# A decoder's last step: routed rows added by index DMAs into the residual, in place of VectorE adds

## The chip, the core and the metric

The kernel runs on one core of a Trainium2 chip. The core has TensorE (PE, matrix multiply), VectorE (DVE, elementwise), ScalarE (ACT, activation functions), GpSimd (POOL, which here makes the index DMAs), and SyncE (SP, which issues plain DMAs). Sixteen DMA engines move data between the chip's main memory and the on-chip memory, whatever queue a transfer was issued on. The metric is the device time of one execution in microseconds (us), as the median of several runs.

## The reference

The program is a two-layer decoder over x of shape (8, 256, 256) in float32: self-attention, cross-attention and a feed-forward part, twice, each added to the residual x. Only the very last part is touched, the second layer's feed-forward part, a mixture of eight experts of which each token uses one, beside a shared expert that all tokens use:

```python
def _L1_ffn_ref(x_bsD, router_DE, w1_eDF, w3_eDF, w2_eFD, ws1_DF, ws3_DF, ws2_FD):
    x_aD = x_bsD.reshape(a, d)
    scores_aE = x_aD @ router_DE
    vals_aK, idx_aK = jax.lax.top_k(scores_aE, K)          # K = 1
    masked_aE = jnp.full_like(scores_aE, -jnp.inf).at[jnp.arange(a)[:, None], idx_aK].set(vals_aK)
    gates_Ea = jax.nn.sigmoid(masked_aE).T
    routed_in_EaD = gates_Ea[:, :, None] * x_aD[None, :, :]
    mid_EaF = silu(einsum('ead,edf->eaf', routed_in_EaD, w1_eDF)) * einsum('ead,edf->eaf', routed_in_EaD, w3_eDF)
    routed_out_EaD = jnp.einsum('eaf,efd->ead', mid_EaF, w2_eFD)
    shared_aD = (silu(x_aD @ ws1_DF) * (x_aD @ ws3_DF)) @ ws2_FD
    return (shared_aD + routed_out_EaD.sum(axis=0)).reshape(b, s, d)

x = x + _L1_ffn_ref(_layernorm(x, axis=-1), ...)
```

So each output row is the sum of three things: the residual row, the shared expert's row, and the row of the one expert to which the token was routed.

## The kernel before

The 2048 tokens are held as 16 tiles of 128 rows by 256 columns, all in one on-chip tile `x` of shape [128, 16, 256]; `x[:, j, :]` is tile j, 128 KB. It is the residual for the whole program. `plain` (line 158) is the program for all ordinary inputs; `token_experts` (line 1740) is its last phase and holds the change.

Routing comes first. The tokens' rows, normalized and multiplied by their gates, are written into the tile `xg` (`gated`, line 1782), and index DMAs on the POOL queue (`put_rows`, line 1842) scatter them to the buffer `xs` in main memory, sorted by expert. The integer table `pos_i` holds for every token the row in that buffer. `slots` (line 1954) then runs the experts over 17 tiles of sorted rows, and `outof` (line 1938) stores each tile's result to `ye` (called `ys` in the profile) from the ScalarE queue. The rows of `ye` are in the sorted order, so that they have to be gathered by `pos_i` to go back to their tokens.

The shared expert runs in four quarters of 512 tokens. For a quarter q, `hidden_shared` makes the hidden activations `mid` in six chunks of up to 128 features (TensorE, then a SiLU on ScalarE at line 1161, then a product on VectorE at line 1162), and `joined(q, mid, i)` (line 1768) multiplies 128 of the tokens out (TensorE, line 1759) and adds the result from the accumulators into `x[:, 4 * q + i, :]` on VectorE (line 1770). Quarters 0 to 2 are done well before; quarter 3 (tiles 12 to 15) is kept to the end, so that TensorE has work while the last expert's rows go out to `ye` and come back.

The end of the program, lines 1985 to 2011, is then this. Sixteen gathers (line 1993, index DMAs on the POOL queue) bring the routed rows of tiles 12, 13, 14, 15, 0, 1, ... 11, in this order, into `xg`, which is free again. All of them wait for the last store to `ye`. On VectorE an order written out by hand runs in four groups: four adds of `xg[:, j, :]` into `x[:, j, :]` (line 2005), then one `joined`. Group 0 adds tiles 12 to 15 and joins tile 12; groups 1, 2, 3 add tiles 0 to 3, 4 to 7, 8 to 11 and join tiles 13, 14, 15. Stores to the output go out on SP: one of four tiles, 512 KB, after the adds of groups 1 to 3 (line 2008), and one of a single tile, 128 KB, after each join (line 2010).

`tc.issue_after(last.ins)` keeps VectorE's instructions of this block behind the last product of quarter 3's hidden activations; it binds instructions on VectorE alone. `tc.manual_schedule(engines=...)` keeps the order in which the program is written on the engines named; on the others a scheduler orders the instructions.

Of the kernel before, what the change touches and what calls it, by code (L numbers as in the profile page):

```python
# [34 lines left out]
ALU = mybir.AluOpType  # L35
# [122 lines left out]
def plain(  # L158
# [4 lines left out]
    nc = tc.nc  # L163
# [6 lines left out]
    x = const.tile([P, NT, D], F32, name="x")  # L170
# [1569 lines left out]
    def token_experts(phase):  # L1740
# [15 lines left out]
        def outward(mid, w2, lo):  # L1756
            ps = mm.tile([P, 2 * D], F32, tag="mm", name="out")[:, :D]
            for i in range(NFC):
                nc.tensor.matmul(ps, mid[:, i, lo : lo + P], w2[:, i, :], start=i == 0, stop=i == NFC - 1)
            return ps  # L1760


        def quarter(q):
            for last in hidden_shared(q, pair, silu):
                pass
            return mid_s[q % 2], last

        def joined(q, mid, i):
            xt = x[:, 4 * q + i, :]
            nc.vector.tensor_tensor(xt, xt, outward(mid, ws2, i * P), ALU.add)  # L1770
# [5 lines left out]
        xg = one.tile([P, NT, D], F32, name="xg")  # L1776
# [208 lines left out]
        ov = out.rearrange("b (t p) d -> (b t) p d", p=P)  # L1985
# [3 lines left out]
        with tc.manual_schedule(engines={mybir.EngineType.PE}):  # L1989
            mid, last = quarter(3)  # L1990
        places = [*range(12, NT), *range(12)]
        for j in places:
            nc.gpsimd.indirect_dma_start(
                out=xg[:, j, :],
                out_offset=None,
                in_=ye[:, :],
                in_offset=bass.IndirectOffsetOnAxis(ap=pos_i[:, j : j + 1], axis=0),
            )

        stored = []  # L2000
        with tc.issue_after(last.ins), tc.manual_schedule(engines={mybir.EngineType.DVE}):
            for i in range(4):
                group = places[4 * i : 4 * i + 4]
                for j in group:
                    nc.vector.tensor_tensor(x[:, j, :], x[:, j, :], xg[:, j, :], ALU.add)  # L2005
                if i:
                    lo = group[0]
                    stored.append(nc.sync.dma_start(ov[lo : lo + 4].rearrange("t p d -> p t d"), x[:, lo : lo + 4, :]))
                joined(3, mid, i)
                stored.append(nc.sync.dma_start(ov[12 + i], x[:, 12 + i, :]))  # L2010
        return stored

    with ExitStack() as phase:
        stored = token_experts(phase)
# [939 lines left out]
```

## Time and profile before

| | us |
|---|---|
| median of 3 runs | 1145.45 (1143.05 to 1147.83) |
| the profiled execution, its own time | 1145.63 |
| its span, first to last instruction | 1143.9 |
| TensorE busy in the span | 1100.9 (96%) |
| VectorE busy | 575.6 (50%) |
| GpSimd busy | 419.3 (37%) |
| the end: first gather issued, after the span's start | 1108.61 |
| the end: last matmul's end | 1134.92 |
| the end: last VectorE instruction, start | 1136.19 |
| the end: last store issued | 1136.97 |

The profile is of one execution. Its times count from the span's start. An engine is busy while it executes; issuing a DMA is not counted as busy for SP and ScalarE, whose DMA issues appear as SPq and ACTq rows in the timeline with the time that the issue took. For POOL the row of an index DMA is the time in which it makes the descriptors. The transfers themselves are seen only in the share of time for which the sixteen DMA engines are busy and in the GB/s that they move. Idle time is put down to what released it.

### The profile page before, as it was taken

The numbers are of one execution on the slowest core, as the hardware profiler recorded it, in microseconds if no ns is written. First come the engines' busy times: TensorE is split into PE (matmuls) and PEld (weight loads), VectorE is DVE, ScalarE is ACT, GpSimd is POOL, SyncE is SP. The second block draws the span as 40 slices with busy tenths as digits, with TensorE's granted clock in tenths as the row PEclk, the third lists the DMA queues.
The fourth block names the chain that finished last, engine by engine and source line by source line (L and its number), as shares of the span: only waits on it lengthen the run. The fifth ranks groups of instructions, "written<-read, shape, count | busy, mean of one in ns | idle before, by whom it ended". The sixth has DMA issues, their size and how long they took to land. (4 is left out here: it accounts for less than half of the span.)

```text
span 1143.9 us, 33749 instructions
## 1 busy us (share of the span) xinstructions
PE 1100.9 (96%) x14706; PEld 702.4 (61%) x14706; DVE 575.6 (50%) x1573; ACT 447.2 (39%) x703; POOL 419.3 (37%) x480
## 2 busy tenths in 40 slices
PE   6979999999999999999999999999999999999996
PEld 3434455555555445667676667676765668888864
DVE  5557889899877446334334243433235572222213
ACT  4657676665444524232323232323233320322220
POOL 3437365546678323242323323242425132000013
PEclk9989999999999999999999999999999999999998
DMA  8082333222004200101010101010121044999924
GB/s 247 2 272 89 105 106 96 86 98 73 18 12 168 84 3 20 39 20 39 20 39 20 39 20 39 20 40 19 40 77 38 1 177 183 387 410 387 367 66 132
DMA packets 52253, 117.15 MB, mean 102 GB/s; under 512 B 8816, under 2 KB 37216, under 8 KB 47744
## 3 DMA queue, kind: packets, MB, share of 16 engines
q1 hardware_dynamic: 45920, 99.17, 25.6%
q0 software_dynamic: 3456, 12.73, 3.0%
q10 hardware_dynamic: 2720, 3.02, 0.7%
q8 instruction: 117, 1.92, 0.7%
q14 instruction: 40, 0.33, 0.1%
HBM read 104.26 MB, written 27.93 MB: 116 GB/s over the span
## 5 line engine op out<-in xcount | busy, mean ns | idle before, releaser
L341 ACT ACTIVATE pT<-st 128x1024 f32<-128x1024 f32 (+1 forms) x128 | 110.5, 915 | 73.9 <-PE st L330 70.0
L367 PE MATMUL o<-pT,padv 128*32 128x256 f32 (+1 forms) x1536 | 96.4, 367 | 7.1 <-DVE by_q L383 5.6
L272 PE MATMUL h<-xrT,w 128*64 128x128 f32 (+1 forms) x1936 | 87.2, 250 | 2.3 <-issue 2.3
L1527 POOL TENSOR_TENSOR both<-pTx 128x512 f32<-128x512 f32 x64 | 80.8, 1291 | 23.1 <-ACT pTx L1525 19.1
L272 PEld LDWEIGHTS h<-xrT,w 128*64 128x64 f32 x1936 | 84.5, 137 | 5.3 <-issue 3.1
L341 ACT ACTIVATE pT<-st,kbias 128x1024 f32<-128x1024 f32 x64 | 67.9, 1112 | 35.9 <-PE st L330 35.9
L1162 DVE TENSOR_TENSOR midr<-sl,h 128x128 f32<-128x128 f32 x102 | 29.4, 288 | 103.5 <-PE h L272 70.8
L367 PEld LDWEIGHTS o<-pT,padv 128*32 128x32 f32 x1536 | 44.6, 110 | 54.6 <-issue 19.1
L1525 ACT ACTIVATE pTx<-stx 128x1024 f32<-128x1024 f32 x64 | 62.1, 1022 | 31.9 <-PE stx L1521 31.9
L1161 ACT ACTIVATE sl<-h 128x128 f32<-128x128 f32 (+1 forms) x114 | 35.4, 310 | 96.8 <-PE h L272 57.8
L330 PE MATMUL st<-qm,kT 32*128 32x512 f32 (+1 forms) x512 | 66.7, 589 | 3.9 <-DVE seq L513 2.2
L254 POOL TENSOR_TENSOR lnrs<-lnve,mhalf 128x2 f32<-128x2 f32 x48 | 36.0, 752 | 91.8 <-DVE lnve L252 85.0
L278 PE MATMUL qk<-xnT,l_wqkv 128*32 128x256 f32 x1024 | 66.9, 383 | 0.0
L1521 PE MATMUL stx<-qTx,kTx 64*128 64x256 f32 x512 | 64.3, 391 | 2.5 <-ACT pTx L1525 2.5
L1561 PE MATMUL ox<-pTx,vx 128*32 128x256 f32 x1024 | 62.3, 380 | 0.0
L1616 POOL TENSOR_TENSOR oT<-oT,rs 128x512 f32<-128x512 f32 x30 | 37.7, 1287 | 66.6 <-DMA rs<-rd 66.6
L1521 PEld LDWEIGHTS stx<-qTx,kTx 64*128 64x128 f32 x512 | 46.1, 186 | 20.7 <-ACT pTx L1525 7.2
L272 PE MATMUL wo<-wout_x,oT 128*64 128x256 f32 x512 | 58.0, 379 | 0.0
L346 POOL TENSOR_SCALAR_AFFINE_SELECT pT<-pT 128x512 f32<-128x512 f32 x64 | 42.1, 673 | 40.6 <-ACT pT L341 40.3
L254 POOL TENSOR_TENSOR lxrs<-lxve,mhalf 128x2 f32<-128x2 f32 x8 | 5.6, 706 | 133.4 <-DVE sc L1300 103.4
L1569 DVE COPY oT<-ox 128x512 f32<-128x512 f32 x16 | 11.1, 691 | 78.9 <-PE ox L1561 78.9
L383 DVE STREAM_TRANSPOSE by_q<-o 128x512 f32<-128x512 f32 x48 | 34.0, 708 | 33.0 <-PE o L367 33.0
(365 smaller groups left out, 2179.6 us busy)
## 6 DMA issues: line engine op xcount, KB each, us to landing
w<-packs SPq DMA_DIRECT2D x22, 1408.0 KB
w<-packs SPq DMA_DIRECT2D x22, 768.0 KB
rs<-rd SPq DMA_DIRECT2D x16, 512.0 KB
packs<-L_ffn_w_eDF SPq DMA_DIRECT2D x8, 704.0 KB
packs<-L_ffn_w_eDF SPq DMA_DIRECT2D x8, 640.0 KB
packs<-L_ffn_w_eFD SPq DMA_DIRECT2D x8, 640.0 KB
wkv_x<-L_xattn_Wkv POOLq DMA_DIRECT2D x1, 4096.0 KB
ctxT<-ctx_T SPq DMA_DIRECT2D x8, 512.0 KB
```

The costliest lines, as they stand in the source:

```text
L254: nc.gpsimd.tensor_tensor(rs[:, :n], ve[:, :n], mhalf[:, :n], ALU.pow)
L272: nc.tensor.matmul(out[h], lhsT[:, h], rhs, start=start, stop=stop, skip_group_check=True)
L278: nc.tensor.matmul(out[h : h + HP], lhsT[:, h : h + HP], rhs, start=start, stop=stop, skip_group_check=True)
L330: nc.tensor.matmul(st[:, r, :, :n], self.kT[rows, c, bass.ts(kt, P)], self.qm[rows, :, c, q0:], start=True, stop=True,)
L341: nc.scalar.activation(pT[:, :, :, :n], st[:, 2 * k : 2 * k + 2, :, :n], AF.Exp, scale=self.scale, **kb)
L346: nc.gpsimd.affine_select(out=pT[:, :, :, :P], in_=pT[:, :, :, :P], compare_op=ALU.is_ge, fill=0.0, base=0, pattern=[[0, 2], [0, 2], [1, P ...
L367: nc.tensor.matmul(o[HP * j : HP * j + HP, m, q0:], self.v_pad[:, kt, 8 * c + 2 * j + m, :], pTs[j // 2][:, j % 2, m, : S - q0], start=kt ...
L1521: nc.tensor.matmul(st[:, g, kt, :], kT[rows, c, bass.ts(kt, P)], qT[rows, c, :], start=True, stop=True)
L1525: nc.scalar.activation(pT, st, AF.Exp, scale=scale)
L1527: nc.gpsimd.tensor_tensor(both, pT[:, :, 0, :], pT[:, :, 1, :], ALU.add)
L1561: nc.tensor.matmul(o[at : at + HP, i, :], v[:, kt, 2 * (c2 + i) + g, lo : lo + HP], pT[:, g, kt, :], start=kt == 0, stop=kt == 1, skip_gro ...
L1616: engines[c2 % 4 // 2].tensor_tensor(oT[:, c2 : c2 + 2, :], oT[:, c2 : c2 + 2, :], rs[:, c2 : c2 + 2, :], ALU.mult)
```

## The change

The sixteen gathers get an operation: each adds the rows that it brings to what lies in its destination, and the destination is now the residual tile `x[:, j, :]` itself, no longer `xg[:, j, :]`. The sixteen adds on VectorE are removed; VectorE's block holds only the four joins. The stores keep their sizes. Each four-tile store now depends on the four gathers of its tiles and no longer on VectorE, and the order of SP's instructions is written out: tiles 0 to 3, then 12, then 4 to 7, then 13, then 8 to 11, then 14, then 15. The order of the gathers on the POOL queue is unchanged.

```diff
         places = [*range(12, NT), *range(12)]
         for j in places:
             nc.gpsimd.indirect_dma_start(
-                out=xg[:, j, :],
+                out=x[:, j, :],
                 out_offset=None,
                 in_=ye[:, :],
                 in_offset=bass.IndirectOffsetOnAxis(ap=pos_i[:, j : j + 1], axis=0),
+                compute_op=ALU.add,
             )
 
         stored = []
-        with tc.issue_after(last.ins), tc.manual_schedule(engines={mybir.EngineType.DVE}):
-            for i in range(4):
-                group = places[4 * i : 4 * i + 4]
-                for j in group:
-                    nc.vector.tensor_tensor(x[:, j, :], x[:, j, :], xg[:, j, :], ALU.add)
-                if i:
-                    lo = group[0]
-                    stored.append(nc.sync.dma_start(ov[lo : lo + 4].rearrange("t p d -> p t d"), x[:, lo : lo + 4, :]))
-                joined(3, mid, i)
-                stored.append(nc.sync.dma_start(ov[12 + i], x[:, 12 + i, :]))
+
+        def shared_rows(i):
+            joined(3, mid, i)
+            stored.append(nc.sync.dma_start(ov[12 + i], x[:, 12 + i, :]))
+
+        def other_rows(lo):
+            stored.append(nc.sync.dma_start(ov[lo : lo + 4].rearrange("t p d -> p t d"), x[:, lo : lo + 4, :]))
+
+        with tc.issue_after(last.ins), tc.manual_schedule(engines={mybir.EngineType.DVE, mybir.EngineType.SP}):
+            other_rows(0)
+            shared_rows(0)
+            other_rows(4)
+            shared_rows(1)
+            other_rows(8)
+            shared_rows(2)
+            shared_rows(3)
         return stored
```

## The prediction

> **What bounds the kernel now.** I read the engines' busy times first, then the chain of waits, then the end of the program in the timeline and in stretches of two microseconds. Everything the change touches lies after 1108 us, so only the last 36 us of the span can move.
>
> ```profile
> span 1143.9 us, 33749 instructions
> PE 1100.9 (96%) x14706; PEld 702.4 (61%) x14706; DVE 575.6 (50%) x1573; ACT 447.2 (39%) x703; POOL 419.3 (37%) x480
> by line: DVE x L1770 0.5%; DVE x L2005 0.5%; issue 0.2%
> ```
>
> TensorE bounds the program as a whole, but the chain that ended last consists of VectorE's adds (line 2005) and joins (line 1770): behind TensorE's last matmul VectorE is late. The chain stops at VectorE's last instruction at 1136.6, though the span ends at 1143.9; the 7.3 us between hold the stores, which the timeline shows:
>
> ```profile
> 1124.40 10.52 PE L1759 MATMUL out<-ws,mid 128*128 128x256 f32 x48
> ...
> 1126.24 1.51 POOL L1993 DMA_INDIRECT xg<-ys,pos_i  x1 [0.30 <-issue]
> 1128.06 0.95 POOL L1993 DMA_INDIRECT xg<-ys,pos_i  x1 [0.31 <-issue]
> 1131.16 0.42 DVE L1770 TENSOR_TENSOR x<-x,out 128x256 f32<-128x256 f32 x1 [3.90 <-PE out L1759]
> 1131.50 1.42 DVE L2005 TENSOR_TENSOR x<-x,xg 128x256 f32<-128x256 f32 x4
> 1131.61 0.35 SPq L2010 DMA_DIRECT2D out<-x  x1
> ...
> 1136.19 0.41 DVE L1770 TENSOR_TENSOR x<-x,out 128x256 f32<-128x256 f32 x1
> 1136.30 0.58 SPq L2008 DMA_DIRECT2D out<-x  x1
> 1136.97 2.03 SPq L2010 DMA_DIRECT2D out<-x  x1
> ```
>
> To be seen here: TensorE ends at 1124.40 + 10.52 = 1134.92, the last join starts only at 1136.19, and no store leaves before 1131.61, because SP's stores stand behind VectorE. Then the stretches (columns: PE, PEld, DVE, ACT, POOL busy, granted clock, DMA share, GB/s):
>
> ```profile
> 1110.00:1120.00 10.00, 10.00 (x24) 4.38 (x24) 1.85 (x3) 1.79 (x3) 7.56 (x9) 1.00 0.36 105
> 1120.00:1130.00 10.00, 10.00 (x37) 6.84 (x36) 2.93 (x7) 1.19 (x2) 7.17 (x7) 1.00 0.35 102
> 1130.00:1132.00 2.00, 2.00 (x11) 1.75 (x10) 0.84 (x3) 0.00 (x0) 0.00 (x0) 1.00 0.08 31
> 1132.00:1134.00 2.00, 2.00 (x11) 1.77 (x10) 2.00 (x7) 0.00 (x0) 0.00 (x0) 1.00 0.27 89
> 1134.00:1136.00 2.00, 0.93 (x5) 0.47 (x3) 2.00 (x7) 0.00 (x0) 0.00 (x0) 1.00 1.02 333
> 1136.00:1138.00 2.00, 0.00 (x0) 0.00 (x0) 0.60 (x2) 0.00 (x0) 0.00 (x0) 1.00 1.04 344
> ```
>
> From 1134 on the DMA engines are full (share 1.0) at 333 to 344 GB/s, while from 1110 to 1134 they are a third busy or less. So the end is bound by 2.1 MB of stores that start late.
>
> Last, the price of a gather now (median and range of a line's instructions, in ns) and what its data costs the engines:
>
> ```profile
> L1993 POOL DMA_INDIRECT xg<-ys,pos_i x16: 946/949/1508, 1108.6 to 1128.1; - x16
> L2005 DVE TENSOR_TENSOR x<-x,xg x16: 414/416/419, 1125.8 to 1135.9; 128x256 f32<-128x256 f32 x16
> q0 software_dynamic: 768, 2.10, 34.2%
> ```
>
> POOL makes a gather in 0.95 us and starts one every 1.254 us (0.95 and the 0.30 of issue). The last line is the gathers' queue between 1110 and 1131: 34.2% of 21 us is 7.2 us of all sixteen engines, 0.45 us a gather. The last gather is issued at 1128.06 and its data is in by 1130.5, 2.45 us later.
>
> **The change part by part.** The sum is made against the profiled execution: span 1143.9, own time 1145.63, which is 0.2 above the median shown (1145.45).
>
> The adds. Sixteen of 0.42 us start 0.335 apart and leave VectorE. Four (tiles 12 to 15) lay under TensorE's matmuls and cost nothing. The other twelve lie between the joins: each group of four with its join takes 1.67 us, three groups run from 1131.50 to 1136.60. Without them the last join waits only for TensorE's 1134.92: start about 1135.03, 1.16 us earlier. The first join still waits for TensorE until 1131.16; I keep that.
>
> The stores of tiles 0 to 3. The eighth gather is issued at 1117.48 and lands near 1119.9, so SP sends 512 KB near 1120, when the DMA engines are about 65% free, and not at 1132.95. This store moves ahead of tile 12's on SP's queue; what stands behind it there (tile 12) waits for its join until 1131.6 anyway. At 338 GB/s (the mean of the two full stretches) it is 1.55 us less in the backlog.
>
> The other stores. SP is in order: tile 12 at 1131.6 (join), 4 to 7 at 1132.0, tile 13 at 1132.5, 8 to 11 at 1132.9, tile 14 at 1133.4 (an issue takes 0.35 to 0.41 where the queue isn't full), tile 15 at 1135.5. The wait that is added is tile 4's to 7's behind tile 12's join: no loss against 1134.85 before. Data follows an issue by about 0.8 us. From 1132.4 the five stores before the last, 1.44 MB, take 4.3 us, to 1136.7; the last adds 0.4: 1137.1. By itself the last one, issued at 1135.5, would need until 1137.3 (the first store before took 1.4 to 1.8). Before, by the same arithmetic, 1.97 MB in one piece from 1133.7 end at 1139.5. Gain: 2.2 to 2.4 us; what follows (receipts, SP's closing waits) is the same in both.
>
> The gathers' new price is not shown by this trace: no DMA here adds. From below it is that of a plain gather, 0.95; a gain in it would only come from the adds no longer running beside POOL (the gather at 1126.24, issued while they ran, took 1.51), at most 0.56 us on a stream that has slack. From above I take twice, with the issue gap kept: cadence 2.2, or 2.5 if the gap doubles too. What the sum makes of it: with cadence c the last gather lands at T = 1108.61 + 15c + 2.45, and behind it go the stores of 8 to 11, 14 and 15 in SP's order: 0.1 + 0.8 + 0.79 MB / 338 GB/s = 3.2 us. Now T is 1129.9, so T + 3.2 = 1133.1, under the 1137.2 of the stores. It stays hidden up to c = 1.53, takes the gain away at 1.68 and makes the kernel 0.5% slower at 2.06.
>
> Here two rules stand against the change. The nearest rows of the trace are POOL's plain loads by size:
>
> ```profile
> L1893 POOL DMA_DIRECT2D xr<-xs x17: 536/538/597, 956.7 to 1054.5; - x17
> L809 POOL DMA_DIRECT2D wout_x<-L_xattn_Wout x1: 955/955/955, 360.0 to 360.0; - x1
> ```
>
> The first moves 128 rows of 1 KB, the second 1024: 896 rows more cost 0.42 us, 0.06 per 128. By that an extra read descriptor per row is nearly free: about 1.0, c = 1.31, all hidden. The Trainium skill, "DMA: Bandwidth & Descriptors", section "SWDGE vs HWDGE vs iDMA", says that a GpSimd core computes a pair of descriptors, one read and one write, for each operation; "Collectives: The Full Stack", section "The bandwidth ceiling", says that an add in the DMA needs two source reads, so two read descriptors per chunk, and halves the rate. Three descriptors for two, if all of the 0.95 scales: 1.42, an estimate, c = 1.73, T = 1137.0, end 1140.2, 0.7 us slower than before (own time 1146.3). I take a value near the trace's rows, at or below 1.2 (c up to 1.5), because they scale so weakly; but an index gather costs 0.41 more than a plain load of the same rows, so its work per row is not free, and the rule stays in the range.
>
> For the data, halved rate makes 0.45 into 0.9 us per gather, an estimate from that page; it fits into 1.254, together with the early store (0.9 x 16 + 1.55 = 16 us of the 20 us stream). It would bound the stream beyond 2.8 times (1.254 / 0.45).
>
> Sum: 1145.63 - 2.3 = 1143.3.
>
> **The rivals.**
> A, as above: 1143.3, bound by TensorE's last matmul and the stores behind it. For it: the idle DMA engines from 1110 to 1134 and the 4 us of slack. Its own range is 1141 to 1146.
> B, POOL becomes the bound: making an adding index gather costs about double. T = 1108.61 + 33 + 2.45 = 1144.1, end 1147.3, 7.8 us after 1139.5: 1153.4; with c = 2.5, 1157.9. For it: 0.95 us for 128 rows, so POOL is already busy three quarters of this stretch and has no second engine to help; sixteen instructions multiply any surcharge. It decides from 2.06, that is 0.8 us more per gather. Against it: how little POOL's loads grow with rows.
> C, the adds are slow in the DMA engines, or each gather must wait for the one before to land (c at least 2.45): read, add and write back of 1 KB rows. From 4.6 times the data cost (2.06 / 0.45), or by the wait, 1152 to 1158 or beyond. Against: the gathers have different tiles as destinations, and now up to two are in flight with no wait beyond reuse.
> D, nothing gained: the early store and the earlier join are hidden, or the early store does not leave early because SP's first wait is satisfied late; then only the join's 1.2 us or nothing: 1144.5 to 1145.6.
>
> **How the numbers follow.** A measurement of this kernel can tell about 0.5%, 5.7 us, from no change. A's gain of 2.3 us lies within that. Chances: A 0.43, D 0.10, B 0.34, C 0.09, and 0.04 for more than 5.7 us of gain, for which the end holds no place (the whole from TensorE's last matmul to the span's end is 9 us, of which most is a join, a store's flight and the closing). So faster 0.04, within 0.53, slower 0.43. The range runs from A with 2.8 us to spare, 1140.5, to B with c = 2.5, 1158.5; below it lies 0.04, above it about 0.13.
>
> **What would show it.** Right: POOL's rows of line 1993 at most 1.2 us and started within 1.53 of each other; the first SP store near 1120; four joins and no other VectorE work after 1126, the last starting near 1135.0; the DMA share full from about 1132.5 to 1137. Wrong: rows of line 1993 above 1.7 us, or gaps between them ended by DMAs, and the store of tiles 8 to 11 issued after 1138, long after the last matmul. If the rows are short and the DMA share between 1110 and 1130 is near 1, it is C.

## The result, and the profile after

| | before | after |
|---|---|---|
| median of 12 runs each, us | 1146.89 | 1151.28 |
| ratio after / before, 95% interval | | 1.0041 (1.0028 to 1.0054) |
| profiled execution: own time / span, us | 1145.63 / 1143.9 | 1150.11 / 1148.4 |
| last matmul's end, us of the span | 1134.92 | 1135.03 |
| from there to the span's end, us | 9.0 | 13.4 |

The changed kernel is slower by 4.4 us, where 2.3 us of gain had been forecast. TensorE ends at the same place in both profiles; the whole loss lies behind it. First the page's span and busy times of the changed kernel, and its chain of waits in the window from 1130 to 1150:

```profile
span 1148.4 us, 33744 instructions
PE 1102.7 (96%) x14706; PEld 702.9 (61%) x14706; DVE 571.0 (50%) x1557; ACT 447.3 (39%) x703; POOL 427.5 (37%) x480
...
by line: POOL x L1993 35.9%; issue 8.8%; POOLq L79 0.1%
```

VectorE does 4.6 us less, POOL 8.2 more, and the chain that ended last, VectorE's adds and joins before, is now POOL's gathers alone (shares of the window). The timeline of the changed kernel's end (start, length, engine, line, operation, and in brackets the idle time before it and what ended it):

```profile
1108.71 1.66 POOL L1993 DMA_INDIRECT x<-ys,pos_i  x1 [52.73 <-DMA ys<-yr]
1110.68 1.57 POOL L1993 DMA_INDIRECT x<-ys,pos_i  x1 [0.30 <-issue]
...
1124.51 10.52 PE L1759 MATMUL out<-ws,mid 128*128 128x256 f32 x48
...
1125.70 0.41 SPq L2008 DMA_DIRECT2D out<-x  x1
1127.30 0.42 DVE L1770 TENSOR_TENSOR x<-x,out 128x256 f32<-128x256 f32 x1 [1.28 <-DMA x<-ys,pos_i]
...
1133.28 0.38 SPq L2008 DMA_DIRECT2D out<-x  x1
1133.76 0.82 SPq L2005 DMA_DIRECT2D out<-x  x1
1134.74 1.55 POOL L1993 DMA_INDIRECT x<-ys,pos_i  x1 [0.30 <-issue]
1135.07 0.42 DVE L1770 TENSOR_TENSOR x<-x,out 128x256 f32<-128x256 f32 x1 [2.17 <-PE out L1759]
1136.59 1.55 POOL L1993 DMA_INDIRECT x<-ys,pos_i  x1 [0.30 <-issue]
1141.10 0.38 SPq L2008 DMA_DIRECT2D out<-x  x1
1141.58 1.44 SPq L2005 DMA_DIRECT2D out<-x  x2
```

To be seen: VectorE is no longer late (the last join starts at 1135.07, 0.04 behind TensorE), but POOL still makes gathers when TensorE is done. The last is issued at 1136.59, 8.5 us later than before, and the store of tiles 8 to 11 can leave only at 1141.10. The stores of tiles 14 and 15, whose rows were complete by 1135.5, stand behind it on SP's queue. The first store leaves at 1125.70.

The gathers themselves: the group's row (ns, shortest/median/longest), the landing line of the view of tile x (us from issue to landing), and the gathers' DMA queue between 1100 and 1150 (packets, MB, share of all sixteen DMA engines):

```profile
L1993 POOL DMA_INDIRECT x<-ys,pos_i x16: 1537/1547/1661, 1108.7 to 1136.6; - x16
DMA to landing us min/median/max: 3.9/4.8/5.7
...
q0 software_dynamic: 2304, 2.10, 30.5%
```

A row costs 1.547 us where it cost 0.949, and with the unchanged 0.30 of issue one starts every 1.85 us. The queue now needs 2304 packets for the sixteen gathers' 2.10 MB, about 0.9 KB each, where before 768 packets carried the same bytes, 2.7 KB each. Its share, 30.5% of 50 us for sixteen gathers, is 0.95 us of all engines per gather, where it was 0.45. The landing takes longer too: the first profile of the kernel before gives no such line, but a later one of the same kernel (the third, below) has

```profile
DMA to landing us min/median/max: 2.7/2.8/4.1
```

The stretches of the changed kernel (PE, PEld, DVE, ACT, POOL busy, clock, DMA share, GB/s):

```profile
1134.00:1136.00 2.00, 1.03 (x5) 0.57 (x3) 0.42 (x1) 0.00 (x0) 1.70 (x2) 1.00 0.96 278
...
1138.00:1140.00 2.00, 0.00 (x0) 0.00 (x0) 0.00 (x0) 0.00 (x0) 0.14 (x1) 0.81 0.78 111
1140.00:1142.00 2.00, 0.00 (x0) 0.00 (x0) 0.00 (x0) 0.00 (x0) 0.00 (x0) 0.50 0.07 12
1142.00:1144.00 2.00, 0.00 (x0) 0.00 (x0) 0.00 (x0) 0.00 (x0) 0.00 (x0) 0.50 1.00 338
```

Before, the DMA engines were full with stores from 1134 to 1138 and beyond. Now they bring the last gathers until about 1140, stand almost empty until SP is released and its first data moves, and are full with the last stores only from 1142.

Behind the stores come the closing instructions of each queue. They have rows too, though the chain of waits does not show them; a DRAIN is one of them. First before, then after:

```profile
L2950 POOLq DRAIN  x3: 46/103/4402, 1132.4 to 1143.6; - x3
L2950 SPq DRAIN  x3: 7/7/13, 1143.0 to 1143.3; - x3
```

```profile
L2957 POOLq DRAIN  x3: 46/103/4402, 1142.6 to 1148.1; - x3
L2957 SPq DRAIN  x3: 7/7/13, 1147.5 to 1147.8; - x3
```

POOL's first DRAIN takes 4.40 us. It starts after POOL's last rows have landed: at 1132.4 before, so it was over by 1136.8, under the stores; at 1142.6 after, so it is over at 1147.0. SP's first DRAIN, which closes the stores, comes at 1143.0 and 1147.5. So in the changed kernel two chains end within half a microsecond of each other, one through the stores and one through POOL's own closing.

### The profile page after: what moved, and what is told of

The parts are those of the page before. It is cut to its first block, busy times and chain, and to the rows that moved or that the text cites. A ratio compares the mean times of both kernels' runs of the same rounds, so it can differ in the third digit from the quotient of the medians.

```text
span 1148.4 us, 33744 instructions
## 1 busy us (share of the span) xinstructions
PE 1102.7 (96%) x14706; PEld 702.9 (61%) x14706; DVE 571.0 (50%) x1557; ACT 447.3 (39%) x703; POOL 427.5 (37%) x480
## 4 chain that ended last, share of the span: by engine, by line
PE 84%; DVE 6%; ACT 3%; issue 2%; POOL 1%; SPq 1%; DMA 1%; POOLq 0%; ACTq 0%; DVEq 0%
PE h L272 7%; PE st L330 7%; PE k L272 6%; PE v L272 6%; PE wo L272 5%; PE o L367 5%; PE ox L1561 5%; PE stx L1521 5%; PE out L1942 4%; PE qk L278 3%; PE h L1169 3%; PE q L272 3%; PE out L1759 3%; PE ao L278 2%; ACT pT L341 2%
```

## The experiments

Every ratio below is to the kernel before, timed on the same chip in the same set of runs.

The theory after the result: the adding operation itself costs the time, by POOL's longer rows and the later landing; leaving out VectorE's adds and sending stores early costs nothing. The rivals: the new order of SP's queue is at fault; it is adding into `x`, with stores and joins beside it; or it is the stores' start alone, which another order on SP would mend.

**The change without the add.** The only edit to the changed kernel:

```diff
                 in_offset=bass.IndirectOffsetOnAxis(ap=pos_i[:, j : j + 1], axis=0),
-                compute_op=ALU.add,
```

> The changed kernel with the add taken out of the gathers: they overwrite the residual tiles, so the residual and shared sums of tiles 0 to 11 and the residual of tiles 12 to 15 are left out of the output. Everything else (VectorE's four joins, SP's written order, early stores) is as changed. Theory 1 (POOL's price for an adding gather is the whole loss): line 1993 back at 0.95 us and one every 1.25 us, the last landed near 1130.5, last store issued near 1135.5, about 2.3 us less than before: ratio 0.997 to 0.999. Theory 2 (SP's written order and the early stores lose the time): still 3 to 5 us slower than before, ratio 1.003 to 1.004.

Measured: 1143.26 us (22 runs) against 1143.27 of before, ratio 0.9993 (0.9982 to 1.0003). The rows of line 1993 are back at 0.946 us, and the end is in this profile 5.8 us behind TensorE:

```profile
1117.38 0.41 SPq L2007 DMA_DIRECT2D out<-x  x1
...
1121.49 10.52 PE L1759 MATMUL out<-ws,mid 128*128 128x256 f32 x48
```

The first store leaves at 1117.38, before the last stage, as the prediction wanted it. So the whole loss goes with the adding operation, and the order on SP's queue costs nothing. But the early stores and the missing adds do not bring 2.3 us either.

**VectorE's adds kept, gathers plain, order changed.** The edit to the kernel before: the sixteen adds stay, but those of tiles 0 to 7 stand ahead of the second join and SP's order is written out. Here `other_rows` holds the four adds of its tiles ahead of their store. The loop that is replaced and the helpers are left out of this cut:

```diff
+        with tc.issue_after(last.ins), tc.manual_schedule(engines={mybir.EngineType.DVE, mybir.EngineType.SP}):
+            add_rows(range(12, NT))
+            shared_rows(0)
+            other_rows(0)
+            other_rows(4)
+            shared_rows(1)
+            other_rows(8)
+            shared_rows(2)
+            shared_rows(3)
```

> Plain gathers into xg and VectorE's sixteen adds kept, but stores and adds reordered: adds of tiles 12 to 15, join 12, adds and stores of 0 to 7, join 13, adds and store of 8 to 11, joins 14 and 15; SP in the same order. Theory 1: POOL is back at 1.25 us a gather, the adds lie under TensorE's last matmuls, the last join starts near 1135.0 and the stores before it have drained: 2 to 3 us less than before, ratio 0.997 to 0.999. Theory 2: stores that leave earlier and in a written order cost time, so no gain or a loss, ratio 1.000 or more.

Measured: 1143.36 us, ratio 0.9996 (0.9985 to 1.0008); the end is 5.9 us behind TensorE. Getting VectorE out of the way needs no adding DMA, but there is nothing measurable to be had from it.

**Adding gathers into the separate buffer, VectorE's adds kept.** The edit to the kernel before:

```diff
                 in_offset=bass.IndirectOffsetOnAxis(ap=pos_i[:, j : j + 1], axis=0),
+                compute_op=ALU.add,
```

> The kernel before with one part of the change alone: the gathers add, but into xg (which still holds the gated rows, so the output has these in addition); VectorE's sixteen adds and the old order of stores stay. Theory 1: 1.55 us and one every 1.85 us on POOL, the last landed near 1141, VectorE's last group and the last join wait for it, the last store leaves near 1143 and the kernel is 0.5 to 2 us slower than the changed one: ratio to before 1.004 to 1.008. Theory 2 (the written order of SP and the early stores are the loss): as fast as before, 0.999 to 1.001.

Measured: 1151.50 us against 1145.75, ratio 1.0041 (1.0028 to 1.0053), the same as the change's. So with the rows added into `xg` in place of `x`, with VectorE's adds kept and with the old order of stores, the loss is the same. In the same set the changed kernel, run again,

> The changed kernel again, beside the variants. Theory 1 (POOL's descriptors for an adding gather, then the last gather's landing, the stores of tiles 8 to 11, 14 and 15, and POOL's own closing after it): the end from the last matmul's end to the span's end is again 13 to 13.5 us. If the kernel before usually has an end of 6 to 7 us, the ratio is 1.0055 to 1.0065; if it has 9 us, 1.004.

gave 1.0035 (1.0024 to 1.0047), with its end again 13.4 us behind TensorE (1137.50 to 1150.9), and the kernel before against itself,

> The kernel before, profiled a second time. In its first profile VectorE's first join of the end waited for TensorE until 1131.16, 4 us after that product's twelve matmuls were through, while in the changed kernel and in both variants with plain gathers the first join started within 0.5 us of them. If that late start belongs to this kernel, it shows again, and the end from the last matmul's end to the span's end is again about 9.0 us. If it belongs to that one execution, the first join starts 3 us after the first matmul of line 1759 and the end is 6 to 7 us: then the prediction's gain of 2.3 us was measured against an end that is usually not there. Ratio 1.000 within 0.001 either way.

gave 1.0008 (0.9993 to 1.0022), so a ratio of that size means no difference here.

**What the add costs POOL.** Behind the kernel before, six kinds of POOL's DMAs, three times each: plain and adding loads of 128 rows of 1 KB, plain and adding index gathers of 128 and of 64 rows. In the cut, `pr` stands for rows of `xg` that are no longer read, and `at_row` and `half_at` take the row numbers from `pos_i`:

```diff
+        for _ in range(3):
+            nc.gpsimd.dma_start(out=pr[:, 0, :], in_=ye[:P, :])
+            nc.gpsimd.dma_start(out=pr[:, 1, :], in_=ye[:P, :], accum_op=ALU.add)
+            nc.gpsimd.indirect_dma_start(out=pr[:, 2, :], ..., in_offset=at_row)
+            nc.gpsimd.indirect_dma_start(out=pr[:, 3, :], ..., in_offset=at_row, compute_op=ALU.add)
+            nc.gpsimd.indirect_dma_start(out=pr[:64, 4, :], ..., in_offset=half_at)
+            nc.gpsimd.indirect_dma_start(out=pr[:64, 5, :], ..., in_offset=half_at, compute_op=ALU.add)
```

> The kernel before with 18 more DMAs on POOL at its end, into rows of xg that are no longer read (nothing of the output changes): plain and adding loads of 128 rows with fixed addresses, plain and adding gathers of 128 rows, and of 64 rows, three of each. Only POOL's rows are read, not the time. If the surcharge belongs to the descriptors of each row, a gather of 64 rows pays half of it (0.3 us) and an adding load with fixed addresses pays it as well (0.54 to about 1.1). If it is a fixed cost of an adding instruction, 64 rows pay the whole 0.6. If it belongs to adding behind an index, the load with fixed addresses pays nothing.

```profile
L2016 POOL DMA_DIRECT2D xg<-ys x3: 561/597/877, 1149.2 to 1156.2; - x3
L2017 POOL DMA_DIRECT2D xg<-ys x3: 864/867/953, 1149.8 to 1158.7; - x3
L2018 POOL DMA_INDIRECT xg<-ys,pos_i x3: 942/976/1027, 1128.0 to 1140.3; - x3
L2019 POOL DMA_INDIRECT xg<-ys,pos_i x3: 1560/1564/1622, 1129.3 to 1141.6; - x3
L2020 POOL DMA_INDIRECT xg<-ys,pos_i x3: 917/920/954, 1131.2 to 1143.5; - x3
L2021 POOL DMA_INDIRECT xg<-ys,pos_i x3: 1425/1425/1427, 1132.5 to 1144.7; - x3
```

By medians, the add costs a plain load 0.27 us (0.867 - 0.597), an index gather of 128 rows 0.59 (1.564 - 0.976) and one of 64 rows 0.51 (1.425 - 0.920). Halving the rows takes away only 0.08 of 0.59. A line through the two sizes, an estimate from two points, gives 0.42 us per instruction and 0.17 per 128 rows. So the surcharge is mostly one of the instruction, and sixteen of them pay it sixteen times. The three samples of a kind are few, but the gathers' lie within 0.09 of each other. The plain loads' spread over 0.32 and reach into the adding ones', so the 0.27 is uncertain.

**The stores as the rows land.** The changed kernel with SP's queue in the order in which its rows become ready, and tiles 8 to 11 stored singly:

```diff
             other_rows(0)
             shared_rows(0)
-            other_rows(4)
             shared_rows(1)
-            other_rows(8)
             shared_rows(2)
+            other_rows(4)
             shared_rows(3)
+            for j in range(8, 12):
+                stored.append(nc.sync.dma_start(ov[j], x[:, j, :]))
```

> The changed kernel with SP's order alone rewritten to when things are ready (tiles 0 to 3, 12, 13, 14, 4 to 7, 15, then 8, 9, 10, 11 one by one). Theory 1: POOL still ends near 1138.1 and the last gather lands near 1141; behind it only 128 KB is left in place of 768 KB, so 1.5 to 2.3 us less than the changed kernel, but still 1.5 to 3 us more than before: ratio to before 1.0015 to 1.0027. Theory 2 (SP's order is the whole of the loss): below before, ratio under 1.000.

Measured: 1151.07 us, ratio to before 1.0063 (1.0049 to 1.0077), so no gain over the change; the profiled span is the same 1148.4, and its end is 13.5 us behind TensorE, for 13.4. The closing rows say why:

```profile
L2958 POOLq DRAIN  x3: 46/103/4402, 1143.2 to 1148.1; - x3
L2958 SPq DRAIN  x3: 7/7/12, 1146.0 to 1147.8; - x3
```

SP closes 1.5 us earlier than in the changed kernel (1146.0 for 1147.5), but POOL's DRAIN runs from 1143.2 to 1147.6, and the span ends 0.8 behind that. Freeing one of the two chains shows the other.

**POOL's closing by itself.** If that chain is real, late POOL DMAs that nobody waits for must delay the end without any add. To the kernel with reordered adds, three more plain gathers into rows that are already read:

```diff
             shared_rows(3)
+        for _ in range(3):
+            nc.gpsimd.indirect_dma_start(
+                out=xg[:, 11, :],
+                out_offset=None,
+                in_=ye[:, :],
+                in_offset=bass.IndirectOffsetOnAxis(ap=pos_i[:, 11:12], axis=0),
+            )
```

> The same kernel with adds first and plain gathers throughout, and behind it three more plain gathers of tile 11's rows into the buffer of gathered rows, which nobody reads any more: they wait for the add of tile 11 and then each for the one before. Nothing of the result depends on them; 384 KB more data. Theory (POOL's closing decides once its last row lands late): the first is issued after tile 11's add, near 1133.5, each later one about 2.5 us behind, last landing near 1141, span's end about 7 us behind it, near 1148: 6 to 7 us slower than adds first, ratio 1.005 to 1.006, although the stores leave and land as in adds first; POOL's DRAIN starts near 1142.5 and takes 4.40. Rival (the stores and the add in the DMA engines were what cost the time; an idle POOL's late DMAs only have to land): end at about 1141 + 1, ratio about 1.000.

Measured: 1153.17 us, ratio 1.0095 (1.0073 to 1.0118).

```profile
1134.06 0.42 DVE L1770 TENSOR_TENSOR x<-x,out 128x256 f32<-128x256 f32 x1 [2.17 <-PE out L1759]
1137.29 0.94 POOL L2024 DMA_INDIRECT xg<-ys,pos_i  x1 [4.84 <-DMA xg<-ys,pos_i]
1140.30 0.94 POOL L2024 DMA_INDIRECT xg<-ys,pos_i  x1 [2.06 <-DMA xg<-ys,pos_i]
...
L2969 POOLq DRAIN  x3: 46/103/4647, 1145.1 to 1150.3; - x3
```

The last join is as early as ever and the last store was issued by 1134.9, yet the span ends at 1150.5. The last gather starts at 1140.30, POOL's DRAIN begins 4.8 us later and takes 4.65. That is 9.4 us over before, more than the 6 to 7 that I had put down: the second of the three gathers starts 5.8 us behind the first (1131.52), not 2.5. The mechanism is the one expected.

**Half and a quarter of the gathers adding.** In the first kernel the gathers of tiles 4 to 11 are plain and VectorE adds those eight:

```diff
-                out=x[:, j, :],
+                out=x[:, j, :] if j not in range(4, 12) else xg[:, j, :],
...
-                compute_op=ALU.add,
+                compute_op=ALU.add if j not in range(4, 12) else ALU.bypass,
```

> The changed kernel with the add in the first eight gathers alone (tiles 12 to 15 and 0 to 3); the last eight are plain into xg, and VectorE adds tiles 4 to 7 and 8 to 11. Theory 1 (a surcharge for each adding gather): eight rows of line 1993 at 1.55 us and eight at 0.95, the last landed near 1134.7, the store of tiles 8 to 11 issued near 1136.3, 4 to 5 us less than the changed kernel: ratio to before 0.999 to 1.001. Theory 2: as slow as the changed kernel, 1.004.

In the second only the first four, of tiles 12 to 15, add; the rest is as in the kernel with reordered adds:

```diff
-                out=xg[:, j, :],
+                out=x[:, j, :] if j >= 12 else xg[:, j, :],
...
+                compute_op=ALU.add if j >= 12 else ALU.bypass,
...
-            add_rows(range(12, NT))
```

> The kernel with the plain gathers and the reordered adds (adds first), but the first four gathers, of tiles 12 to 15, add into the residual rows themselves, so VectorE has twelve adds left. Theory (the end is the later of two chains: TensorE's last matmul + about 5.9 us through joins, stores and SP's closing, and POOL's last landing + about 7 us through POOL's own closing, whose DRAIN takes 4.40 us): four rows of 1.55 and twelve of 0.95 put the last gather at about 1129.8 and its DRAIN's start near 1134.8 (adds first: last gather 1128.5, DRAIN 1133.5), so the DRAIN ends near 1139.2, before SP is done; ratio to before 0.998 to 1.001, span about 5.9 us after TensorE's end. Rival (every adding gather costs a sixteenth of the 4.4 us, wherever it stands): 1.1 us slower, ratio 1.001, DRAIN not decisive. Rival (adding gathers of any number slow the landing of the later plain ones, as the kernel of eight and eight seemed to show): joins or stores late again, ratio 1.002 or more.

Both came out slower than the theory had it: the half 1147.77 us, ratio 1.0037 (1.0024 to 1.0051), for 0.999 to 1.001; the quarter 1145.07 us, ratio 1.0013 (1.0003 to 1.0024), for 0.998 to 1.001. The half's end:

```profile
1133.05 1.01 POOL L1993 DMA_INDIRECT xg<-ys,pos_i  x1 [0.30 <-issue]
1136.26 0.43 DVE L2009 TENSOR_TENSOR x<-x,xg 128x256 f32<-128x256 f32 x1 [2.53 <-DMA xg<-ys,pos_i]
1138.20 0.43 DVE L2009 TENSOR_TENSOR x<-x,xg 128x256 f32<-128x256 f32 x1 [1.52 <-DMA xg<-ys,pos_i]
```

The quarter's:

```profile
1126.86 1.03 POOL L1993 DMA_INDIRECT xg<-ys,pos_i  x1 [0.30 <-issue]
1129.60 0.42 DVE L2005 TENSOR_TENSOR x<-x,xg 128x256 f32<-128x256 f32 x1 [1.52 <-DMA xg<-ys,pos_i]
1131.81 0.43 DVE L2005 TENSOR_TENSOR x<-x,xg 128x256 f32<-128x256 f32 x1 [1.78 <-DMA xg<-ys,pos_i]
1132.15 0.74 DVE L1770 TENSOR_TENSOR x<-x,out 128x256 f32<-128x256 f32 x2
```

In both the last plain gather lands about 5 us after its issue (1133.05 to 1138.20, 1126.86 to 1131.81), where plain gathers in the kernel before have a median of 2.8 and a longest of 4.1 in the third profile, and VectorE's last adds wait for it. By then the four-tile stores are on the DMA engines. In the quarter POOL's DRAIN runs from 1133.4 to 1137.8 and SP's first one comes at 1138.8, so POOL's closing does not decide; the last two joins, which end at 1132.9, do. The interval also covers the even share of a sixteenth each (1.001), so its time doesn't tell those two apart; the waits in its timeline speak for the late landing. That the stores cause the late landing fits both timelines, but no run held the stores back to show it.

**Is there 2.3 us to be had?** The prediction read its gain from one profile, in which the first join waits until 1131.16, 6.8 us after TensorE began the stage. The kernel before was profiled again on three chips:

> The kernel before, unchanged, one more profile of it. Question: is the late first join (1131.16 and 1131.14 in the two profiles, where TensorE's first quarter of the last stage is done by about 1127) a property of this kernel's end or of single executions? Theory (property): first join again near 1131, at least 6 us after TensorE began the last stage, span's end 8 us or more after TensorE's last matmul. Rival (single executions): join about 2.8 us after TensorE began the stage, as in the changed kernel, and the end about 6 to 7 us after the last matmul.

> The kernel before, unchanged. Theory (the late join comes with the chip): the first join's place, near 2.9 us after TensorE began the last stage or 4 us and more later, is the same in this profile as in the next one of the same chip, and goes with the chip's median of the kernel before (about 1143.5, or about 1146). Rival (single executions): the two may differ.

> The kernel before, unchanged, once more on the same chip: as the run ahead of it says.

The run that the prediction used has a twin, the second profile (the run of the kernel before against itself):

```profile
1127.38 8.47 PE L1759 MATMUL out<-ws,mid 128*128 128x256 f32 x38 [1.02 <-issue]
1131.14 0.42 DVE L1770 TENSOR_TENSOR x<-x,out 128x256 f32<-128x256 f32 x1 [2.46 <-PE out L1759]
```

The third profile does not show it:

```profile
1126.12 10.52 PE L1759 MATMUL out<-ws,mid 128*128 128x256 f32 x48
1129.00 0.42 DVE L1770 TENSOR_TENSOR x<-x,out 128x256 f32<-128x256 f32 x1
...
1136.68 0.42 DVE L1770 TENSOR_TENSOR x<-x,out 128x256 f32<-128x256 f32 x1 [0.83 <-PE out L1759]
1137.13 0.33 SPq L2010 DMA_DIRECT2D out<-x  x1
```

Here the first join starts 2.9 us into the stage, the last 0.04 us behind TensorE's end, and the span ends 6.4 us behind it, at 1143.0. The fourth and fifth profiles, on another chip, have the same 2.9 us and 6.2 and 6.4. Beside those two the variant without the add was timed once more:

> The changed kernel without its adding operation, once more, beside profiles of the kernel before on the same chip. Theory (the late first join of the kernel before, seen in two of its three profiles, comes with the chip: where the kernel before takes about 1146 it has it, where it takes about 1143.5 it does not): if this chip's kernel before shows late joins, this kernel is 2 to 3 us faster than it here, ratio 0.997 to 0.998, as the prediction's sum said; if it shows joins in time, ratio 0.999 to 1.000. Rival (the late join is a property of single executions and averages out): ratio 0.999 to 1.000 either way.

It gave 0.9993 (0.9981 to 1.0006) again. In the sets whose profiles hold the first join back, the kernel before took 1145.75 and 1146.89 us; in those whose profiles do not, 1143.79 and 1144.24. That the late join comes with the chip fits this, but five profiles do not prove it, and no set timed the variant without the add where the join is held back. There the forecast gain may exist; on the two chips where the variant ran it does not show.

## Why the prediction was wrong

A gain of 2.3 us was forecast and a loss of 4.4 came. Case A, held likeliest, did not occur: POOL became the bound of the end, as in rival B, but with a price below B's double. The range reached the measured time only by its part for B.

- **The price of a gather** is the step that failed. I put it at or below 1.2 us, with c up to 1.5, by the plain loads that grow by 0.06 us per 128 rows. It measured 1.547 and a cadence c of 1.85, past the break-even of 1.68 that I had worked out. The row by which I chose bears on rows; the surcharge is mainly one of the instruction, as the run of six kinds shows (0.51 of 0.59 remains at half the rows). Three descriptors for two, from the Trainium skill ("DMA: Bandwidth & Descriptors", "SWDGE vs HWDGE vs iDMA", with "Collectives: The Full Stack", "The bandwidth ceiling"), had given 1.42, an estimate, and was nearer, though a surcharge for each row's descriptors would have halved with the rows, and the measured one does not. The halved data rate of the second page agrees with the traces: 0.95 us per gather for 0.45, where 0.9 was the estimate.
- **The landing** was the second term mis-sized. The formula kept the 2.45 us read from the end of a plain gather's data. The last gather starts at 1136.59 and SP is released at 1141.10, so it took about 4.4. With both measured terms the prediction's own sum closes: 1108.61 + 15 x 1.85 + 4.4 = 1140.8, and 3.2 more is 1144.0, 4.5 after 1139.5, so an own time of 1150.1; the profiled execution took 1150.11. The landing comes from that same profile, so the sum shows that the two terms suffice, and is no second test of them. With the measured c alone it would have been 1148.1.
- **"What follows is the same in both"** held in its number by luck. POOL's closing was over 6 us before SP's first DRAIN and is now over 0.5 us before it. It adds nothing here only because the stores end about as late; it is why the reordered stores gained nothing and why the three late gathers that nobody reads cost 9.4 us.
- **The base** of 2.3 us of gain: "The first join still waits for TensorE until 1131.16; I keep that.". In the changed kernel it starts at 1127.30, and three of five profiles of the kernel before don't have that wait either. With it, the kernel before ends 9.0 us behind TensorE (8.4 in the second profile), and the change's 13.4 is 4.4 later, as measured in the first set. Without it the end is 6.2 to 6.4, so the change should lose about 7 us there, an estimate from the ends. It was not timed there itself; the kernel with stores as the rows land, which ends as late behind TensorE, was 7.2 us slower (0.0063 x 1143.27) in a set whose kernel before was as fast as where the join is in time.
- **The stores of tiles 0 to 3** left at 1125.70, not near 1120, since the eighth gather came late for the same reason.
- **What held:** TensorE's end and the last join (1135.07 for 1135.03), the gathers' gap of 0.30, no wait of one gather for another (C), and the sign named for being wrong, a store of tiles 8 to 11 after 1138 (1141.10). Rows above 1.7 us, the other sign, were set too high: 1.55 was enough.

## What to carry to other kernels

An operation that moves from a half-idle engine into DMAs of a serial maker has to be priced by the maker's instruction, times how many there are, and by when the last lands; leaving out VectorE's sixteen adds brought nothing measurable on the two chips where that was timed. If the price is not in the trace, measure it with a few extra instructions behind a kernel before moving sixteen, and let a break-even that lies within the range of prices speak against the move. A gain of a few microseconds read from one profile's end needs a second profile, and every queue's closing belongs to the end, the makers' too.

## What the runs showed that I had not expected

- POOL's DRAIN took 4.40 us in fourteen profiles, 4.65 with three more index gathers and 5.87 with eighteen more POOL DMAs; as long as POOL's last rows land early enough it is free.
- Adding gathers go as packets of about 0.9 KB, where plain ones, with the same rows and bytes, go at 2.7 KB on average, and land after 3.9 to 5.7 us for 2.7 to 4.2 in the kernel before.
- With eighteen more DMAs on POOL, TensorE itself ran in pieces: its last matmuls came singly, with gaps "issue" of up to 1.75 us, and the last join started at 1149.19. What held TensorE and VectorE back here, and VectorE's first join in two of the five profiles of the kernel before, is open: POOL's plain gathers ran at that time in all of these profiles, also in those without the wait.

```profile
1133.76 0.38 PE L1759 MATMUL out<-ws,mid 128*128 128x256 f32 x1 [0.24 <-issue]
1135.88 1.19 PE L1759 MATMUL out<-ws,mid 128*128 128x256 f32 x3 [1.75 <-issue]
1138.71 0.42 DVE L1770 TENSOR_TENSOR x<-x,out 128x256 f32<-128x256 f32 x1 [11.47 <-remote]
```
